# Layer 0 in a front and a back part, three operations moved between engines, and the dense products in one stream

## The chip, the cores and the metric

The kernel runs on one core of a Trainium2 chip. A core has TensorE (PE, matrix products into PSUM), VectorE (DVE), ScalarE (ACT), GpSimd (POOL) and SyncE (SP, which issues transfers). Each engine works through its own queue in order and waits on semaphores for the others. The metric is the device time of one launch in microseconds, lower is better.

## The reference, cut to what matters

Two layers on x of 4 batches x 512 tokens x 256 features, all in float32:

```python
xn = layernorm(x)
# layer 0
q, k, v = xn @ Wq.T + bq, xn @ Wk.T + bk, xn @ Wv.T + bv
ctx  = (elu(q) + 1) * cumsum((elu(k) + 1) * v, over tokens) * 0.25
attn = ctx @ Wo.T + bo
xr   = rms(xn) * norm_w
vals, idx = top_k(xr @ Wc.T / temperature, 32)      # of 512
e    = softmax(vals) @ genes[idx]                   # 32 wide
x    = x + attn + tanh(e @ Wd.T) * xr * (e @ Wu.T) * scale
# layer 1
xn   = layernorm(x)
q, k, v = split(rms(xn) @ w_qkv.T); q, k = rms(q), rms(k); w = exp(k)
y    = sigmoid(q) * cumsum(w * v) / (cumsum(w) + 1e-6)
u, g = split(y @ w_swiglu.T)
a    = xn + (u * silu(g)) @ w_out.T
# two of 16 experts per token, and a shared expert for all
f    = sum over the 2 best experts of weight * swiglu(xn @ w_gate_up[e]) @ w_down[e]
f   += swiglu(xn @ shared_gate_up) @ shared_down
x    = x + a + f
```

## The kernel before

The tokens lie on the 128 partitions; a batch is four tiles of 128 tokens (NT = 4), the residual stream xs stays in the on-chip memory for the whole launch. Every product is done twice over in passes, so that one call of T.matmul appears as two matmuls in the profile.

The work comes as Python generators, each yield ending a step. together() (line 43) draws from several generators in turn, in proportion to the number of steps that each is said to have. What it makes is the order of the program; the framework then places the instructions into the engines' queues, with that order as the priority, and may bring a ready instruction forward.

**layer0(b, i0, nt)** (line 224) is layer 0 for nt tiles of a batch: statistics (bn_stats, line 201; a square root on ACT, line 207; a reciprocal), normalise (line 213, on DVE) to xn, transposes to xnT, then per tile logits (line 286) and top (line 296: four rounds of V.max and V.match_replace over 512 values, then exp into a tile e and a masking product), between them the parts of the attention: attend_kv (phi of k, v, a cumulative scan on DVE, line 271) and attend_q (phi of q, and the context product on DVE, line 280, with the factor QSCALE), then express (line 313: transposes of e, products with genes and with Wd and Wu, tanh, and five products and sums, four of them on POOL) and out (line 336: the output projection, added to xs).

**mix(b, i0, nt)** (line 361) is the attention of layer 1 and the choice of experts: statistics and normalise to xn1, transposes to xn1T, the projections (line 384), copies of q and k on ACT, vs on DVE (line 393), squares, exponentials, transposes and scans (line 421), reciprocals (line 430) and the product yT (line 432), then the expert scores and their two best. Its results go to made[(b, i0)].

**dense(b, half, busy)** (line 566) is, for 256 tokens, everything that is the same for all of them: 11 chunks, three of the shared expert (inputs xn1T, weights sgu and sdn) and eight of the gated product (inputs yT, weights wugt and wot1). A chunk is up (eight matmuls of 256 columns into a PSUM tile gu, tanh on ACT at line 582, a DVE product at line 584, and then, if busy, a copy on ACT and a product on POOL at lines 586 and 587, else one DVE product at line 589) and down (four matmuls into acc at line 595), which follows two chunks behind its up. After the eleventh chunk the two last downs follow at once, and acc, of which there is one buffer (ps_a), is added to xs.

**The stages** (lines 633 to 678): layer 0 of batch 0's first half alone; then mix of it beside layer 0 of the second half; then three stages that each combine a mix, the layer 0 of the next batch and one half of the dense products; then mix of batch 3 beside dense(1, 1) and the loading of the expert weights. After that the routing (route, which works out a row for every token and expert), beside six steps of the dense products of batch 2; the scatter (line 544: 32 indirect transfers issued on POOL, each after the last down emitted before it, see paced, line 92) beside 15 steps of them; and the rest of them. Then come the experts (line 772), each pair of row blocks fetched from xrows on SP (line 709), and last the dense products of batch 3, beside the gathering of the experts' results (line 804) and their addition to xs (line 815).

SP issues the loads of x and of the weights in the order of the program: x of batch 0, the weights of layer 0, those of layer 1 (lines 136 to 147), then x of batches 1 to 3.

Of the kernel before, what the change touches and what calls it, by code (L numbers as in the profile page):

```python
# [53 lines left out]
def tile_two_layers(  # L54
# [79 lines left out]
    nc.sync.dma_start(wot, wo0.rearrange("(h p) e -> p h e", p=P))  # L134

# [12 lines left out]
    for b in range(1, B):  # L148
        load_x(b)
# [5 lines left out]
    for h in range(NH):  # L155
        V.tensor_scalar(wct[:, h], wct[:, h], nwc[:, h : h + 1], None, ALU.mult)
    rtemp = wp.tile([P, 1], F32, name="rtemp")
# [28 lines left out]
    one = first.enter_context(tc.tile_pool(name="one0", bufs=1, side="right"))  # L186
# [7 lines left out]
    def statistics(pool, b, i0, nt):  # L194

        mv = pool.tile([P, NT, 2], F32, name="mv")
        rs = pool.tile([P, 2, NT], F32, name="rs")
        ve = pool.tile([P, NT], F32, name="ve")
        for i in range(nt):
            bs = pool.tile([P, 6], F32, name="bs")  # L200
            V.bn_stats(bs, xs[:, b, i0 + i])
            V.bn_aggr(mv[:, i], bs)
        V.tensor_scalar(rs[:, 0, 0:nt], mv[:, 0:nt, 1], LN_EPS, None, ALU.add)
        V.reciprocal(ve[:, 0:nt], rs[:, 0, 0:nt])
        V.tensor_tensor(ve[:, 0:nt], ve[:, 0:nt], mv[:, 0:nt, 1], ALU.mult)
        V.tensor_scalar(rs[:, 1, 0:nt], ve[:, 0:nt], RMS_EPS, None, ALU.add)
        S.activation(rs[:, :, 0:nt], rs[:, :, 0:nt], AF.Sqrt)
        V.reciprocal(rs[:, :, 0:nt], rs[:, :, 0:nt])
        return mv, rs

    def normalise(to, b, i0, nt, mv, rs):
        for i in range(nt):
            V.tensor_scalar(
                to[:, i], xs[:, b, i0 + i], mv[:, i, 0:1], rs[:, 0, i : i + 1], ALU.subtract, ALU.mult
            )
# [8 lines left out]
    def layer0(b, i0, nt):  # L224

        W = nt * P
        mv, rs = statistics(io, b, i0, nt)
        xn = io.tile([P, NT, D], F32, name="xn")
        normalise(xn, b, i0, nt, mv, rs)

        sl = io.tile([P, 2, NT], F32, name="sl")
        V.tensor_scalar(sl[:, 0, 0:nt], rs[:, 1, 0:nt], rtemp, None, ALU.mult)
        V.tensor_scalar(sl[:, 1, 0:nt], rs[:, 1, 0:nt], scl, None, ALU.mult)
        yield
        xnT = io.tile([P, NH, L], F32, name="xnT")
        for h in range(NH):
            S.copy(xnT[:, h, 0:W], turn(xn, nt, h * P))
        yield


        def project(c):
            pm = bank()[:, 0:W]
            for h in range(NH):
                T.matmul(  # L244
                    pm,
                    wqkv[:, h, c * P : (c + 1) * P],
                    xnT[:, h, 0:W],
                    start=(h == 0),
                    stop=(h == NH - 1),
                )  # L250
            return pm

        def phi(c):

            pm = project(c)
            e = io.tile([P, L], F32, name="phi", bufs=3)[:, 0:W]
            S.activation(e, pm, AF.Relu, bias=nbqk[:, c : c + 1], scale=-1.0)
            S.activation(e, e, AF.Exp, scale=-1.0)
            V.scalar_tensor_tensor(e, pm, bqkv1[:, c : c + 1], e, ALU.add, ALU.max)
            return e  # L260

        ctxT = one.tile([P, NH, L], F32, name="ctxT")
        cums = {}

        def attend_kv(h):
            fk = phi(2 + h)
            pv = project(4 + h)
            kv = one.tile([P, L], F32, name="kv")[:, 0:W]
            V.scalar_tensor_tensor(kv, pv, bqkv[:, 4 + h : 5 + h], fk, ALU.add, ALU.mult)
            cum = io.tile([P, L], F32, name="cum")[:, 0:W]  # L270
            V.tensor_tensor_scan(
                cum, ones[:, 0:W], kv, carry[:, h : h + 1] if i0 else 0.0, ALU.mult, ALU.add
            )
            if i0 + nt < NT:
                V.tensor_copy(carry[:, h : h + 1], cum[:, W - 1 : W])
            cums[h] = cum

        def attend_q(h):
            fq = phi(h)
            V.scalar_tensor_tensor(ctxT[:, h, 0:W], fq, QSCALE, cums[h], ALU.mult, ALU.mult)  # L280


        rden = io.tile([P, NT], F32, name="rden")
        exT = one.tile([P, L], F32, name="exT")

        def logits(i):
            pl = bank()
            for h in range(NH):
                T.matmul(  # L289
                    pl, xnT[:, h, i * P : (i + 1) * P], wct[:, h], start=(h == 0), stop=(h == NH - 1)  # L290
                )
            lg = io.tile([P, NG], F32, name="lg")
            S.copy(lg, pl)  # L293
            return lg

        def top(i, lg):
            tp = io.tile([P, NACT], F32, name="top")
            rep = io.tile([P, NG], F32, name="rep")
            for r in range(NACT // 8):
                src = lg if r == 0 else rep  # L300
                V.max(tp[:, 8 * r : 8 * r + 8], src)  # L301
                V.match_replace(rep, tp[:, 8 * r : 8 * r + 8], src, TAKEN)  # L302
                if r == 0:
                    nm = io.tile([P, 1], F32, name="nm")
                    V.tensor_scalar(nm, tp[:, 0:1], sl[:, 0, i : i + 1], -1.0, ALU.mult, ALU.mult)
                    e = io.tile([P, NG], F32, name="e")
                    S.activation(e, lg, AF.Exp, bias=nm, scale=sl[:, 0, i : i + 1])
            den = io.tile([P, 1], F32, name="den")
            V.scalar_tensor_tensor(e, rep, TAKEN, e, ALU.is_equal, ALU.mult, accum_out=den)
            V.reciprocal(rden[:, i : i + 1], den)  # L310
            return e

        def express(i, e):
# [8 lines left out]
            S.copy(exT[:, i * P : (i + 1) * P], px[:, 0:P])  # L322
            du = bank()
            T.matmul(du, exT[:, i * P : (i + 1) * P], wdut, start=True, stop=True)  # L324
# [8 lines left out]
            G.tensor_tensor(xs[:, b, i0 + i], xs[:, b, i0 + i], bob, ALU.add)  # L333
            G.tensor_tensor(xs[:, b, i0 + i], xs[:, b, i0 + i], dn, ALU.add)

        def out(i):
# [5 lines left out]
            V.tensor_tensor(xs[:, b, i0 + i], ao, xs[:, b, i0 + i], ALU.add)  # L342


        parts = [lambda h=h, f=f: f(h) for h in range(NH) for f in (attend_kv, attend_q)]
        lg = logits(0)
        for i in range(nt):
            nxt = logits(i + 1) if i + 1 < nt else None
            e = top(i, lg)
            yield  # L350
            for part in parts[i * len(parts) // nt : (i + 1) * len(parts) // nt]:
                part()
            yield
            express(i, e)
            lg = nxt
            yield
        for i in range(nt):
# [3 lines left out]
    def mix(b, i0, nt):  # L361
# [17 lines left out]
        for i in range(nt):  # L379
# [13 lines left out]
            V.tensor_scalar(vs[:, i], pv[:, 0:D], rs[:, 1, i : i + 1], None, ALU.mult)  # L393
# [172 lines left out]
    def dense(b, half, busy):  # L566


        unit = (b, 2 * half) if (b, 2 * half) in made else (b, 0)
        t0 = (2 * half - unit[1]) * P  # L570
        ins = [a[:, :, t0 : t0 + HB] for a in made[unit]]
        acc = ps_a.tile([P, 2, D], F32, name="acc")

        def up(gw, g0, uw, u0, m, which, dw, dc):
# [10 lines left out]
            if busy:  # L585
                S.copy(hid[0:m], gu[0:m, 1])  # L586
                G.tensor_tensor(hid[0:m], hid[0:m], th[0:m], ALU.mult)  # L587
            else:
                V.tensor_tensor(hid[0:m], gu[0:m, 1], th[0:m], ALU.mult)
            return hid  # L590

        def down(n, hid):
            m, dw, dc = chunks[n][4], chunks[n][6], chunks[n][7]
            for t in range(2):
# [8 lines left out]
            beat.append(mm.ins.name)  # L603

        hids = []
        for n, c in enumerate(chunks):
            hids.append(up(*c))
            if n >= 2:
                down(n - 2, hids[n - 2])
            yield  # L610
        for n in (NC - 2, NC - 1):
            down(n, hids[n])
        here = xs[:, b, 2 * half : 2 * half + 2]
        V.tensor_tensor(here, acc, here, ALU.add)
        yield


    def chain(*parts):
        for part in parts:
            yield from part  # L620

    H = NC + 1

    def a(b, i0, nt):
        return layer0(b, i0, nt), 2 + 4 * nt

    def m(b, i0, nt):
        return mix(b, i0, nt), 6 + nt

    def d(b, half, busy=True):  # L630
        return dense(b, half, busy), H

    together(a(0, 0, 2))
    together(m(0, 0, 2), a(0, 2, 2))

# [4 lines left out]
    together(m(0, 2, 2), a(1, 0, 4), d(0, 0))  # L640
    together(m(1, 0, 4), a(2, 0, 4), d(0, 1))
    together(m(2, 0, 4), a(3, 0, 4), d(1, 0))
# [27 lines left out]
    together(m(3, 0, 4), d(1, 1), (load_experts(), 17))  # L670
    mixing.close()
    routing = ctx.enter_context(ExitStack())
    d2 = chain(dense(2, 0, False), dense(2, 1, False))
    together((route(), 8), (islice(d2, 6), 6))
    routing.close()

    together((scatter(), 33), (islice(d2, 15), 15))
    run_all(d2)
# [121 lines left out]
    for step, _ in enumerate(chain(dense(3, 0, False), dense(3, 1, False))):  # L800
# [11 lines left out]
        while added < 2 * NTT and 9 * added <= 16 * (step - 4):  # L812
# [61 lines left out]
```

## Time and profile before

| | us |
|---|---|
| three runs, median (lowest, highest) | 592.69 (591.28, 592.82) |
| the profiled execution | 585.74 |
| its span, from the first to the last instruction | 583.9 |

| engine | busy us | share of the span |
|---|---|---|
| PE | 536.5 | 92% |
| DVE | 375.4 | 64% |
| ACT | 233.3 | 40% |
| POOL | 171.7 | 29% |

In the profile a line such as "L578" is a line of the kernel, "gu<-yT,wugt" the tile written and the tiles read, "x512" the number of instructions. The rows of digits cut the span into 40 slices of 14.6 us and give the busy share in tenths (PEclk: the clock granted to PE). The chain of waits is followed back from the last instruction, each step to what released it. The layer stages fill the first 341 us, routing and scatter the next 60, the experts 402 to 522, the last dense products the rest.

### The profile page before, as it was taken

Reading aid. Unit: us, or ns where it says so; the run is one execution under the profiler, and the core shown is the slowest. Engines: PE = TensorE matmul, PEld = TensorE weight load, DVE = VectorE, ACT = ScalarE, POOL = GpSimd, SP = SyncE. Lnnn points to the kernel's source line nnn. Section 1 sums busy time; section 2 is a strip of 40 time slices with the busy share of each in tenths; the row PEclk is TensorE's granted clock in tenths of the full one; section 3 lists DMA queues with packets and bytes.
Section 4 is the critical chain, followed back from the end, with each engine's and each line's share of the span. In section 5 each row is a group of like instructions: output and inputs, shape, how many; then the busy total and the mean of one; then the engine's idle time right before and its main releaser. Section 6 shows DMA issues by size and latency. Waiting matters only on the chain.

```text
span 583.9 us, 7339 instructions
## 1 busy us (share of the span) xinstructions
PE 536.5 (92%) x2384; PEld 393.1 (67%) x2384; DVE 375.4 (64%) x992; ACT 233.3 (40%) x528; POOL 171.7 (29%) x214
## 2 busy tenths in 40 slices
PE   3557999989999999999999999997999999999997
PEld 1334656557555776566777878884777777788886
DVE  4979999998796897968962696331222222225663
ACT  2454745651655716458154511112333333321111
POOL 1234232343222523224251324771000000007760
PEclk9788999999999999999999999998999999999999
DMA  6993000000000000000056611324333333114540
GB/s 164 382 378 137 1 1 1 2 0 1 1 1 0 0 1 2 0 1 1 2 154 193 184 65 54 105 104 135 91 109 108 109 109 99 55 65 116 146 144 28
DMA packets 38453, 47.39 MB, mean 81 GB/s; under 512 B 4016, under 2 KB 34960, under 8 KB 38160
## 3 DMA queue, kind: packets, MB, share of 16 engines
q1 hardware_dynamic: 35344, 38.53, 20.7%
q0 software_dynamic: 3072, 8.39, 4.7%
q8 instruction: 20, 0.33, 0.2%
q14 instruction: 17, 0.14, 0.1%
HBM read 28.30 MB, written 18.61 MB: 80 GB/s over the span
## 4 chain that ended last, share of the span: by engine, by line
PE 53%; DVE 23%; POOL 8%; issue 6%; ACT 6%; DMA 3%; SPq 0%; POOLq 0%; ACTq 0%; DVEq 0%
PE gu L578 10%; PE pu L738 10%; PE py L759 7%; PE acc L595 6%; PE pm L384 5%; PE pt L701 4%; POOL xrows L544 3%; PE pm L244 3%; DVE sums L430 3%; POOL ys L804 3%; DVE rep L302 3%; DVE top L301 3%; PE pm L289 2%; DVE sums L421 2%; PE pm L324 2%
## 5 line engine op out<-in xcount | busy, mean ns | idle before, releaser
L578 PE MATMUL gu<-yT,wugt 128*128 128x256 f32 x512 | 125.6, 382 | 0.0
L578 PEld LDWEIGHTS gu<-yT,wugt 128*128 128x128 f32 x512 | 95.2, 190 | 19.4 <-issue 7.4
L582 ACT ACTIVATE th<-gu 128x256 f32<-128x256 f32 (+1 forms) x88 | 33.3, 382 | 120.0 <-PE gu L578 116.8
L804 POOL DMA_INDIRECT ys<-yrows,slot x32 | 30.4, 949 | 142.0 <-DMA yrows<-yg 129.6
L595 PE MATMUL acc<-wot,hid 128*128 128x256 f32 x256 | 65.3, 382 | 3.1 <-POOL hid L587 2.4
L738 PE MATMUL pu<-wex,xgT 128*128 x188 | 65.0, 468 | 0.8 <-DMA xg<-xrows 0.8
L584 DVE SCALAR_TENSOR_TENSOR th<-th,gu 128x256 f32<-128x256 f32 (+1 forms) x88 | 35.9, 411 | 41.4 <-ACT th L582 41.4
L587 POOL TENSOR_TENSOR hid<-hid,th 128x256 f32<-128x256 f32 (+1 forms) x44 | 33.6, 768 | 95.7 <-ACT hid L586 95.7
L595 PEld LDWEIGHTS acc<-wot,hid 128*128 128x128 f32 x256 | 48.0, 190 | 13.3 <-POOL hid L587 4.5
L747 DVE TENSOR_TENSOR hb<-pu,hb 128x176 f32<-128x176 f32 x47 | 16.0, 341 | 55.7 <-ACT hb L746 55.7
L244 PE MATMUL pm<-xnT,wqkv 128*128 128x512 f32 (+1 forms) x120 | 46.6, 528 | 4.9 <-ACT lg L293 1.9
L384 PE MATMUL pm<-w,xn1T 128*128 128x512 f32 (+1 forms) x128 | 45.5, 498 | 0.0
L578 PE MATMUL gu<-xn1T,sgu 128*128 128x256 f32 (+1 forms) x192 | 45.2, 380 | 0.0
L759 PE MATMUL py<-wex,hgT 128*128 x188 | 44.5, 379 | 0.0
L759 PEld LDWEIGHTS py<-wex,hgT 128*128 128x128 f32 x188 | 35.7, 190 | 8.6 <-issue 0.2
L738 PEld LDWEIGHTS pu<-wex,xgT 128*128 128x128 f32 x188 | 32.5, 193 | 11.2 <-ACT xgT L715 1.0
L384 PEld LDWEIGHTS pm<-w,xn1T 128*128 128x128 f32 x128 | 24.6, 193 | 21.9 <-issue 18.2
L244 PEld LDWEIGHTS pm<-xnT,wqkv 128*128 128x128 f32 x120 | 23.7, 202 | 22.6 <-issue 13.7
L578 PEld LDWEIGHTS gu<-xn1T,sgu 128*128 128x128 f32 (+1 forms) x192 | 34.1, 181 | 6.6 <-issue 0.9
L751 DVE COPY hgT<-pt 128x512 f32<-128x512 f32 (+1 forms) x24 | 16.3, 680 | 34.3 <-PE pt L701 34.3
L544 POOL DMA_INDIRECT xrows<-xn,slot x32 | 30.9, 966 | 19.6 <-DVE cpair L538 9.7
L301 DVE MAX8 top<-rep 128x8 f32<-128x512 f32 x48 | 32.8, 685 | 0.4
(162 smaller groups left out, 879.6 us busy)
## 6 DMA issues: line engine op xcount, KB each, us to landing
xrows<-zero SPq DMA_DIRECT2D x1, 6016.0 KB, 22.6
xg<-xrows SPq DMA_DIRECT2D x23, 256.0 KB, 2.7
yrows<-yg SPq DMA_DIRECT2D x23, 256.0 KB, 2.1
wex<-in_w_gate_up_dram SPq DMA_DIRECT2D x8, 704.0 KB, 4.6
xs<-in_x_dram SPq DMA_DIRECT2D x4, 512.0 KB, 7.9
wugt<-in_wug_dram SPq DMA_DIRECT2D x1, 2048.0 KB, 12.4
wex<-in_w_down_dram SPq DMA_DIRECT2D x4, 512.0 KB, 5.1
out_dram<-xs SPq DMA_DIRECT2D x7, 256.0 KB, 2.8
```

The costliest lines, as they stand in the source:

```text
L244: T.matmul(pm, wqkv[:, h, c * P : (c + 1) * P], xnT[:, h, 0:W], start=(h == 0), stop=(h == NH - 1),)
L301: V.max(tp[:, 8 * r : 8 * r + 8], src)
L384: T.matmul(o[:, 0:n], xnT[:, h, i * P : (i + 1) * P], w1[:, h, at : at + n], start=(h == 0), stop=(h == NH - 1),)
L544: sc = G.indirect_dma_start(out=xrows, out_offset=bass.IndirectOffsetOnAxis(ap=slot[:, k, i : i + 1], axis=0), in_=xn1[:, i // NT, i % NT] ...
L578: T.matmul(gu[0:m, k], w[:, h, at : at + m], ins[which][:, h], start=(h == 0), stop=(h == NH - 1))
L582: S.activation(th[0:m], gu[0:m, 0], AF.Tanh, scale=0.5)
L584: V.scalar_tensor_tensor(th[0:m], th[0:m], 1.0, gu[0:m, 0], ALU.add, ALU.mult)
L587: G.tensor_tensor(hid[0:m], hid[0:m], th[0:m], ALU.mult)
L595: mm = T.matmul(acc[:, t], hid[0:m, t * P : (t + 1) * P], dw[0:m, dc], start=(n == 0 and t == 0), stop=(n == NC - 1), skip_group_check=True,)
L738: T.matmul(pg[:, 0 : 2 * NI], xT[:, i, h], wex[:, bass.ds(at[i] + h * 2 * NI, 2 * NI)], start=(h == 0), stop=(h == NH - 1),)
L759: mm = T.matmul(py[:, i * D : (i + 1) * D], hT[:, i, h], wex[:, bass.ds(at[i] + EW - (2 - h) * D, D)], start=(h == 0), stop=(h == 1),)
L804: G.indirect_dma_start(out=ys[:, asked], out_offset=None, in_=yrows, in_offset=bass.IndirectOffsetOnAxis(ap=slot[:, k, n : n + 1], axis=0) ...
```

## The change

Layer 0 becomes two generators. front(b, wide) does a whole batch: statistics, xn, xnT, all logits (kept in lg, six buffers), the attention up to the context. back(b, i0, nt) does the top-32, express and out for some of its tiles. Fronts of batches 0 and 1 run ahead of the first dense products and take their projections' PSUM from the tiles gu (wide). Batch 0's back and mix are still in halves. The scan no longer needs a carry in layer 0; cum has one buffer instead of two, kv takes the place of phi's tile, exp works in place on lg, exT is a tile of its own.

xn (in both layers) and vs go from DVE to ACT, for which statistics works out -mean times the reciprocal deviation with one small DVE operation more. The context product goes from DVE to POOL, QSCALE into wot once at the start. x of batch 1 is loaded ahead of layer 1's weights.

The dense products are one generator over all eight halves: down follows two chunks behind up across the halves' ends, and acc is added as soon as the eleventh down is emitted. The choice between POOL and DVE for the second product goes by a flag that is set before routing. Of its 88 chunks 3 + 2 + 3 + 9 + 2 + 3 + 2 + 9 + 2 + 5 = 40 are placed in the mixing, 5 beside route, 15 beside scatter, 6 behind, and 22 at the end; before, it was 44 in the mixing, 22 from routing to the experts and 22 at the end. The pace of the last additions is set anew for 22 steps instead of 24.

```diff
+    load_x(1)
     w1 = const.tile([P, NH, 3 * D + NE], F32, name="w1")
...
-    for b in range(1, B):
+    for b in range(2, B):
         load_x(b)
...
+    S.mul(wot, wot, QSCALE)
...
+        V.scalar_tensor_tensor(mv[:, 0:nt, 0], mv[:, 0:nt, 0], -1.0, rs[:, 0, 0:nt], ALU.mult, ALU.mult)
         return mv, rs
...
-            V.tensor_scalar(
-                to[:, i], xs[:, b, i0 + i], mv[:, i, 0:1], rs[:, 0, i : i + 1], ALU.subtract, ALU.mult
+            S.activation(
+                to[:, i], xs[:, b, i0 + i], AF.Identity, bias=mv[:, i, 0:1], scale=rs[:, 0, i : i + 1]
             )
...
+    def front(b, wide):
...
+            if wide:
+                pm = ps_d.tile([P, 2, HB], F32, name="gu").rearrange("p i c -> p (i c)")
+            else:
+                pm = bank()
...
+            kv = phi(2 + h)
             pv = project(4 + h)
+            V.scalar_tensor_tensor(kv, pv, bqkv[:, 4 + h : 5 + h], kv, ALU.add, ALU.mult)
+            cums[h] = io.tile([P, L], F32, name="cum", bufs=1)
+            V.tensor_tensor_scan(cums[h], ones, kv, 0.0, ALU.mult, ALU.add)
...
-            V.scalar_tensor_tensor(ctxT[:, h, 0:W], fq, QSCALE, cums[h], ALU.mult, ALU.mult)
+            G.tensor_tensor(ctxT[:, h], fq, cums[h], ALU.mult)
...
+        for h in range(NH):
+            for i in (2 * h, 2 * h + 1):
+                logits(i)
+                yield
+            attend_kv(h)
+            yield
+            attend_q(h)
+            yield
+
+    def back(b, i0, nt):
...
+        top(i0)
+        yield
+        for i in range(i0, i0 + nt):
+            if i + 1 < i0 + nt:
+                top(i + 1)
+                yield
+            express(i)
             yield
+        for i in range(i0, i0 + nt):
             out(i)
             yield
...
-            V.tensor_scalar(vs[:, i], pv[:, 0:D], rs[:, 1, i : i + 1], None, ALU.mult)
+            S.activation(vs[:, i], pv[:, 0:D], AF.Identity, scale=rs[:, 1, i : i + 1])
...
+        for half in range(2 * B):
...
+            for n, c in enumerate(chunks):
+                behind.append((half, n, up(ins, bool(calm), *c)))
+                if len(behind) > 2:
+                    down(*behind.pop(0))
+                yield
...
+    f0, f1 = front(0, True), front(1, True)
+    b0 = back(0, 0, 2)
+    run_all(islice(f0, 4))
+    together(some(f0, 6), some(b0, 2))
+    together(some(b0, 4), some(f1, 2))
+    m0 = mix(0, 0, 2)
+    next(m0)
+    run_all(islice(f1, 3))
+    together((m0, 7), some(f1, 5))
...
+    together((back(0, 2, 2), 6), d(3))
+    m0 = mix(0, 2, 2)
+    next(m0)
+    run_all(islice(dd, 2))
+    together((m0, 7), d(3))
+    together((back(1, 0, NT), 12), (front(2, False), 10), d(9))
+    m1 = mix(1, 0, NT)
+    next(m1)
+    run_all(islice(dd, 2))
+    together((m1, 9), (back(2, 0, NT), 12), (front(3, False), 10), d(3))
+    m2 = mix(2, 0, NT)
+    next(m2)
+    run_all(islice(dd, 2))
+    together((m2, 9), (back(3, 0, NT), 12), d(9))
...
+    together((m3, 9), d(5), (load_experts(), 17))
     mixing.close()
     routing = ctx.enter_context(ExitStack())
+    calm.append(True)
+    together((route(), 8), d(5))
     routing.close()
+    together((scatter(), 33), d(15))
+
+    run_all(islice(dd, 6))
...
-        while added < 2 * NTT and 9 * added <= 16 * (step - 4):
+        while added < 2 * NTT and 17 * added <= 32 * (step - 3):
```

## The prediction

> **What bounds it now.** I read engine totals first, then the slices, then busy time by stretch, then the chain of waits where the stretches show a hole.
>
> ```profile
> span 583.9 us, 7339 instructions
> PE 536.5 (92%) x2384; PEld 393.1 (67%) x2384; DVE 375.4 (64%) x992; ACT 233.3 (40%) x528; POOL 171.7 (29%) x214
> PE   3557999989999999999999999997999999999997
> DVE  4979999998796897968962696331222222225663
> PEclk9788999999999999999999999998999999999999
> ```
>
> PE (TensorE) is above nine tenths from the sixth slice (14.6 us each) on; only the first four or five have room. But 92% is not 92% at peak: one 128x256 matmul is listed at 382 ns, while the chain shows how closely they follow:
>
> ```profile
> 86.54 1.29 PE gu L578 x6
> 98.51 2.63 PE pm L384 x8
> 137.87 1.73 PE gu L578 x8
> ```
>
> Eight 256-wide ones take 1.73 us, 216 each; the eight of L384 (four 512 wide, four 272 wide) 2.63, so 430 and 230. Priced so (L738 296, transposes 109 ns, 0.22 us for one tile's eight small ones of L321), the 2384 matmuls are 512 us of work in a span of 584: **72 us lost**, idle or at a low clock. By start times, 35.7 are gone at 60 us, 40.4 at 85, 58.2 at 341, 65.2 at 410, and hardly any in the experts (410 to 520). The stretches say why:
>
> ```profile
> 0.00:30.00 30.00, 14.31 (x44) 8.32 (x45) 21.14 (x72) 9.16 (x18) 6.35 (x17) 0.89 0.85 275
> 30.00:60.00 30.00, 19.21 (x68) 11.54 (x67) 26.53 (x88) 15.02 (x35) 11.13 (x15) 0.84 0.69 242
> 60.00:90.00 30.00, 27.52 (x131) 18.52 (x129) 29.84 (x94) 19.04 (x40) 8.39 (x12) 0.99 0.00 1
> 90.00:190.00 100.00, 95.97 (x397) 60.66 (x398) 86.73 (x228) 52.12 (x118) 32.14 (x41) 1.00 0.00 1
> 341.00:398.00 57.00, 56.70 (x263) 49.00 (x261) 29.68 (x75) 8.05 (x21) 33.20 (x39) 1.00 0.21 74
> 398.00:402.00 4.00, 0.63 (x4) 0.42 (x4) 0.42 (x1) 0.28 (x1) 0.00 (x0) 0.98 0.61 174
> ```
>
> Columns: length, then PE, weight loads, DVE (VectorE), ACT, POOL busy, clock, DMA. To 60 us PE has 33.5 of 60, at a granted 0.84 to 0.89, while DVE has 47.7: the top-32 search (four rounds of L301 and L302, starting 0.66 us apart, some 6.2 us a tile) keeps PE from work. The dense products fill PE once they exist; the first on yT starts at 84.7. To 341 us PE has 283 of work and DVE 280 busy: nearly tied. At 398 PE stands again, and the chain tells for what:
>
> ```profile
> 395.57 2.41 DMA xrows<-xn,slot
> 399.05 3.30 DMA xg<-xrows
> 402.36 2.71 PE pu L738 x4
> ```
>
> The last scatter is issued at 395.57, the fetch waits for it, and the expert matmuls for the fetch; the dense chunks have run out at 397.5.
>
> **Start, the largest part.** Before, batch 0's first half must pass layer0 and mix before any chunk can run, beside the second half's top-32. After, PE has the fronts of two batches to run meanwhile. A front is 24 projections and 16 logits at 430 ns and 8 transposes: 18.1 us. Two of them 36.2; back(0,0,2) 2 x 2.4 (4 transposes, L321, 2 x 430, 4 x 216); mix(0,0,2) 2 x 3.5; the three shared chunks, which need xn1T alone, 3 x 2.59. Together 55.8 us of work without yT. When is yT there? DVE needs f0's statistics 3, two top-32 12.4, f0's phi, kv and scans 6.2, dn and out 1.9, f1's statistics and phi 9.2, mix up to yT 13.5 (2 statistics, 11.5 scans, reciprocals, products): 46. It begins at 4.3, the first lg is at 14 now (one larger statistics chain: say 14.5), and the serial stretch from the second top-32 to exp(k) (8.7 us from the end of L309 at 29.7 to xs at 38.4 now, then statistics, square root, qkv, squares, root, exp) leaves holes that f1 fills only in part. I take 72 for yT instead of 84.7. If PE ran all 55.8 by then, 16 would be lost; I take 22 (it starts near 10.8, and f1's statistics come after two top-32), against 40.4 lost before. The gain is **18**, bounds 8 and 24. Part is clock: in 23 to 29.8, 40 to 46.9 and 57 to 60.5 the granted clock was 0.5 and PE busy 12.6, so 6.3 were lost by it, after idle stretches of 5 and 5.8 us.
>
> load_x(1) goes ahead of the seven weight loads from w1 on in SP's queue: 0.43 us of issue, and 0.5 MB at the 381 GB/s of that stretch is 1.4 us for w1, whose first matmul is at 48.9. Hidden. The multiplication of wot is one 512-wide ACT (0.62, L637).
>
> **Engines changed in the mixing.**
>
> ```profile
> L213 DVE TENSOR_SCALAR xn<-xs,mv,rs 128x256 f32<-128x256 f32 x32 | 15.2, 525 | 0.2
> L410 ACT ACTIVATE qk<-qk,cf 128x256 f32<-128x256 f32 x16 | 8.0, 509 | 0.0
> L280 DVE SCALAR_TENSOR_TENSOR ctxT<-phi,cum 128x512 f32<-128x512 f32 x6 | 4.1, 688 | 0.1
> L368 POOL TENSOR_TENSOR xs<-xs,xn 128x512 f32<-128x512 f32 x2 | 2.6, 1322 | 8.2 <-DVE xn L213 8.2
> ```
>
> DVE loses L213 15.2, vs (L393) 7.6 and the context product 4.1 + 1.6: 28.5. It gains one small product per statistics, 9 x 0.2 = 1.8. ACT's normalise has two pointer operands; L410, SBUF to SBUF with one, is the near row: 32 x 509 = 16.3. The Trainium skill ("ScalarE: Activation LUTs", What ACT_TABLE_LOAD costs) adds about 93 ns for each pointer operand: 32 x 602, an estimate of 19.3. vs costs 16 x 473 (L326) = 7.6. ACT goes from 173 busy of 341 to 197 or 200; either sum fits, and I take the row. Square roots stay one per statistics, and the same table switches (1.28 us) with them.
>
> The skill speaks against the product on POOL: "GPSIMD Engine Reference", Engine selection, puts elementwise two-input work on VectorE, GPSIMD being about 2x slower. The rows agree (1322 against 688): the engines' sum grows. "SBUF — State Buffer", two separate sides, is worse: the two share a port pair as an exclusive lock, the loser waiting out the whole instruction. By the rule 8 x 1.32 = 10.6 of DVE could be blocked. The trace:
>
> ```profile
> 68.60 0.73 POOL L412 TENSOR_TENSOR vs<-vs,qk 128x256 f32<-128x256 f32 x1 [15.60 <-ACT qk L410]
> 68.71 0.65 DVE L408 TENSOR_SCALAR cf<-cf 128x2 f32<-128x2 f32 x1
> ```
>
> L408 ends with the POOL operation; undisturbed it takes 0.15. But most DVE operations here read PSUM or one operand, and L213, which pays it most (525 mean, 384 least: 4.5 us), goes. Between 0 and 10.6 I take 4.
>
> Sum to 341: DVE 280 - 28.5 + 1.8 + 4 - 1.6 (four chunks less) = 256; PE 283 - 10.4 = 272. So DVE drops below PE. But top-32 is put off: after the start DVE has some 210 left and PE 222, 0.95, where from 85 to 341 it was 208 to 238, 0.87. The mixing lost 17.8 there; I charge **4 more**, bounds -4 and 14.
>
> **Chunks beside routing.** The same 33 chunks lie between the third mixing and the experts: 11 + 22 before, 7 + 26 after. But of the 26 chunks 67.3 us stand beside routing and scatter, where 22 gave 57. Scatters follow each other at 1.265 us (0.96 and 0.30 issue), 40.5 for 32; from the start of routing, 341.5, to the first takes 14.2, and to the first fetched rows 60.5. After, that ends 6.8 before the chunks do. The 3.4 us idle, the half clock behind it (0.5 in 402 to 405) and the serial first pair lose 6.8 now: **gain 5**, bounds 0 and 7.
>
> **One stream.** down(10) of a half no longer follows its own up at once (0.64 us idle at 549.4); seven such places: gain 1 to 3. Against it, the next half's first down waits for DVE's addition on the single acc with one up (1.73 us) between instead of three. Addition 0.68 and its hand-over fit if DVE is free. Net **gain 1**, bounds -3 and 3. In the last part the additions follow their gathers by 2.2 to 3 chunks instead of about 4; gather and landing take 1.3 + 3.3, within 5.8 us, so nothing.
>
> **Sum:** 18 - 4 + 5 + 1 = 20. The profiled execution took 585.7 (span 583.9 and 1.8 around it): 565.7. The runs' median is 592.7, 7 above that execution, and the forecast is for such runs: 592.7 - 20, rounded down to **572**.
>
> **Rivals.** *VectorE takes it back.* Mix 1, back 2 and front 3 come together with 5 chunks: about 60 us of DVE, 55 of PE. If mix waits there and in the next stage, 12 of the start's gain return: 584. For it: DVE at 29.84 of 30 after the start. Against: 28.5 us less in sum.
>
> *The order doesn't arrive.* Queue order isn't program order (L441's memset, late in the program, ran at 2.00 us): chunks may be pulled forward, the scatter gap stay and half the start's gain fail: 592.7 - 9 + 3 = 587.
>
> *Slower: POOL's queue.* cum has one buffer; the second scan of a front waits on DVE for the context product of the first half, and POOL takes its queue in order. Ahead of a product can stand dn or hid, whose waits were 47.9 us in 12 and 95.7 in 27, some 4 each, 12.6 at most. Behind the scan stand phi and the next top-32. At 4 for each of 8 the loss is 32, the sum 12 slower: 605. From 2.5 us per product the gain is gone. Against: POOL is 29% busy, and DVE's queue can have other work placed ahead of the scan.
>
> **Chances.** Forecast 0.57, VectorE 0.16, order 0.09, POOL's queue 0.15, nothing measurable (within 0.3%, 1.8 us, what this kernel's measurement tells from none) 0.03. The forecast's own range is 560 to 581; the first two rivals reach 590, and 557 takes in the start's upper bound. Faster: 0.57 and nearly all of 0.25.
>
> **What will show it.** Right: PE busy over 42 in the first 60 us, first yT chunk before 75; no idle PE between dense and pu; DVE's sum near 353; lost time near 52. Wrong: a scan waiting on ctxT, hid waits grown, DVE full with PE under 90% from 100 to 280, chunks spent before the scatter ends.

## The result, and the profile after

The changed kernel is slower: 600.48 us (597.45 to 601.21) against 592.24 us (591.28 to 592.82) of the kernel before, measured beside it, a ratio of 1.0135, 95% interval 1.0117 to 1.0153. The forecast was 572 us. Measured again later, beside its variants, it took 591.80 us (590.90 to 592.08) against 587.50, a ratio of 1.0076 (1.0059 to 1.0092).

The page of the changed kernel, with the same rows as before:

```profile
span 597.2 us, 7258 instructions
PE 538.2 (90%) x2360; PEld 388.1 (65%) x2360; DVE 352.2 (59%) x930; ACT 255.0 (43%) x566; POOL 176.9 (30%) x218
PE   2958898999999989899899399879999999999987
DVE  2899999598874859934932983232222222225563
PEclk9998999999999999999989889999999999999999
```

DVE's sum fell by 23 us, as worked out (353 was forecast). But PE's row has a 3 in its 23rd slice (328 to 343 us), where it had a 9 before, and the granted clock (PEclk) has an 8 in the 24th. By stretches (length, then PE, weight loads, DVE, ACT, POOL busy, clock, DMA):

```profile
0.00:30.00 30.00, 19.52 (x43) 8.82 (x44) 17.00 (x51) 13.53 (x22) 6.97 (x17) 1.00 0.78 271
30.00:60.00 30.00, 20.89 (x76) 10.24 (x74) 29.29 (x92) 20.90 (x37) 9.61 (x12) 0.94 0.70 245
90.00:190.00 100.00, 95.25 (x419) 65.67 (x418) 74.33 (x212) 57.64 (x124) 39.23 (x50) 1.00 0.00 1
333.00:350.00 17.00, 7.25 (x21) 5.64 (x20) 15.03 (x22) 0.38 (x1) 2.29 (x7) 0.70 0.00 0
```

In the first 60 us PE is busy 40.4 instead of 33.5: the start did gain, but under the 42 named in the prediction. From 90 to 190 DVE has a quarter of its time free, and PE is no fuller than before. From 333 to 350 PE stands for more than half of the time, while DVE is busy 15 of 17 us. What DVE does there is told by the timeline of the same execution (start, duration, instruction, idle time before and its releaser), first DVE, then PE, and then DVE of the kernel before at the same place, cut to four lines:

```profile
332.29 1.21 DVE L426 TENSOR_TENSOR_SCAN sums<-ones,pm 128x512 f32<-128x512 f32 x1
333.42 3.34 DVE L435 RECIPROCAL sums<-sums 128x256 f32<-128x256 f32 x2
336.68 0.63 DVE L433 SCALAR_TENSOR_TENSOR sums<-pm,sums 128x512 f32<-128x512 f32 x1
337.22 0.68 DVE L437 TENSOR_TENSOR yT<-sums 128x512 f32<-128x512 f32 x1
337.82 3.36 DVE L435 RECIPROCAL sums<-sums 128x256 f32<-128x256 f32 x2
341.09 1.16 DVE L426 TENSOR_TENSOR_SCAN sums<-ones,pm 128x512 f32<-128x512 f32 x1
342.17 0.40 DVE L589 SCALAR_TENSOR_TENSOR th<-th,gu 128x256 f32<-128x256 f32 x1
```

```profile
332.34 1.46 PE L583 MATMUL gu<-yT,wugt 128*128 128x256 f32 x6
343.56 1.22 PE L603 MATMUL acc<-wot,hid 128*128 128x256 f32 x2 [9.75 <-DVE hid L591]
```

```profile
331.75 3.34 DVE L430 RECIPROCAL sums<-sums 128x256 f32<-128x256 f32 x2
335.01 0.36 DVE L584 SCALAR_TENSOR_TENSOR th<-th,gu 128x256 f32<-128x256 f32 x1
...
338.71 0.41 DVE L584 SCALAR_TENSOR_TENSOR th<-th,gu 128x256 f32<-128x256 f32 x1
339.03 3.36 DVE L430 RECIPROCAL sums<-sums 128x256 f32<-128x256 f32 x2
```

From 329.5 to 342.2 DVE's queue holds only the scans, reciprocals and products of mix(3). The first th (L589), which a dense chunk needs before its PSUM tile comes free, is behind them; before, a th stood between the reciprocals. Three chunks wait for their th, one in each of the three tiles gu. PE's next instruction is a down (L603) that needs the hid (L591) made from that th, so PE stands for 9.75 us. The granted clock is 0.57 from 343.5 to 350 us, just behind that. L591 is the second product of the chunks emitted after the flag is set, so the chunks that wait are already those placed behind the mixing, and the 40 placed in it have been used up.

Priced as in the prediction (216 ns for a 256-wide matmul, and so on), both kernels have the same 512 to 513 us of PE work; what is lost beside it, by stretch, in us:

| stretch | before (span 583.9) | changed, first execution (597.2) | changed, second execution (590.0) | second minus before | forecast |
|---|---|---|---|---|---|
| to 80 | 40.0 | 31.3 | 31.5 | -8.5 | -18 |
| 80 to 330 | 16.8 | 25.5 | 25.1 | +8.3 | +4 |
| 330 to 360 | 1.7 | 13.6 | 13.3 | +11.6 | none |
| 360 to 420 | 6.4 | 7.6 | 1.5 | -4.9 | -5 |
| 420 to the end | 6.2 | 6.5 | 5.9 | -0.3 | -1 |

At 330 us both kernels have lost the same, 57 us: what the start gains is gone again by the end of the mixing.

The two executions of the changed kernel differ in one stretch. In the first, ACT began several of its th 3 to 6 us after their gu between 370 and 395 us; the second shows nothing of it, nor does any variant. Why it came is open, and the experiments are read against the second.

### The profile page after: what moved, and what is told of

It reads as the page before. It is cut to its first block, busy times and chain, and to the rows that moved or that the text cites. A ratio compares the mean times of both kernels' runs of the same rounds, so it can differ in the third digit from the quotient of the medians.

```text
span 597.2 us, 7258 instructions
## 1 busy us (share of the span) xinstructions
PE 538.2 (90%) x2360; PEld 388.1 (65%) x2360; DVE 352.2 (59%) x930; ACT 255.0 (43%) x566; POOL 176.9 (30%) x218
## 4 chain that ended last, share of the span: by engine, by line
PE 56%; DVE 28%; ACT 6%; issue 3%; DMA 3%; POOL 3%; SPq 0%; another core or an unknown queue 0%; DVEq 0%; ACTq 0%; POOLq 0%
PE gu L583 16%; PE pu L767 9%; PE acc L603 9%; PE py L788 7%; DVE rep L312 5%; DVE top L311 5%; PE pm L389 4%; PE pt L730 3%; DVE sums L435 3%; DVE sums L426 3%; PE pm L224 2%; PE pm L334 1%; DVE lg L318 1%; DMA wqkv<-in_wqkv_dram 1%; DVE bs L203 1%
## 5 line engine op out<-in xcount | busy, mean ns | idle before, releaser
L583 PEld LDWEIGHTS gu<-yT,wugt 128*128 128x128 f32 x512 | 96.8, 192 | 17.9 <-ACT hid L593 3.4
L603 PE MATMUL acc<-wot,hid 128*128 128x256 f32 x256 | 68.7, 386 | 13.4 <-DVE hid L591 11.8
L589 DVE SCALAR_TENSOR_TENSOR th<-th,gu 128x256 f32<-128x256 f32 (+1 forms) x88 | 36.1, 413 | 71.8 <-ACT th L587 60.1
L767 PE MATMUL pu<-wex,xgT 128*128 x188 | 63.8, 461 | 0.8 <-ACT xgT L744 0.8
L603 PEld LDWEIGHTS acc<-wot,hid 128*128 128x128 f32 x256 | 47.4, 192 | 21.4 <-DVE hid L591 12.6
L594 POOL TENSOR_TENSOR hid<-hid,th 128x256 f32<-128x256 f32 (+1 forms) x40 | 29.7, 751 | 64.0 <-ACT hid L593 63.9
L583 PE MATMUL gu<-xn1T,sgu 128*128 128x256 f32 (+1 forms) x192 | 47.8, 383 | 0.4 <-DVE phi L264 0.4
L389 PE MATMUL pm<-w,xn1T 128*128 128x512 f32 (+1 forms) x128 | 44.0, 493 | 0.5 <-ACT xn1T L377 0.5
L283 PE MATMUL pm<-wct,xnT 128*128 128x512 f32 x64 | 32.5, 641 | 1.1 <-ACT xnT L242 1.1
L311 DVE MAX8 top<-rep 128x8 f32<-128x512 f32 x48 | 32.6, 680 | 0.2
L312 DVE MATCH_REPLACE8 rep<-top,rep 128x512 f32<-128x512 f32 x48 | 32.3, 674 | 0.0
```

The lines of the kernel that those rows point to most:

```text
L283: T.matmul(pl, xnT[:, h, i * P : (i + 1) * P], wct[:, h], start=(h == 0), stop=(h == NH - 1))
L389: T.matmul(o[:, 0:n], xnT[:, h, i * P : (i + 1) * P], w1[:, h, at : at + n], start=(h == 0), stop=(h == NH - 1),)
L583: T.matmul(gu[0:m, k], w[:, h, at : at + m], ins[which][:, h], start=(h == 0), stop=(h == NH - 1))
L589: V.scalar_tensor_tensor(th[0:m], th[0:m], 1.0, gu[0:m, 0], ALU.add, ALU.mult)
L603: mm = T.matmul(acc[:, t], hid[0:m, t * P : (t + 1) * P], dw[0:m, dc], start=(n == 0 and t == 0), stop=(n == NC - 1), skip_group_check=True,)
L767: T.matmul(pg[:, 0 : 2 * NI], xT[:, i, h], wex[:, bass.ds(at[i] + h * 2 * NI, 2 * NI)], start=(h == 0), stop=(h == NH - 1),)
```

## The experiments

They ran in four groups, each on a chip of its own and beside the kernel before: e1 to e4, then c0 and e5 to e7, then e8 to e11, then e12 to e14. The kernel before took 587.05 to 587.50 us in each. Across groups the ratios are compared. The times expected for e1 to e4 start from the 600.5 us of the first measurement, so they too are judged by the ratios and the traces. "44, 26, 18" means the number of chunks placed in the mixing, from routing to the experts, and at the end; the changed kernel has 40, 26, 22.

| label | edit to the changed kernel | us | ratio to before (95%) |
|---|---|---|---|
| c0_after | none | 591.80 | 1.0076 (1.0059-1.0092) |
| e1_44_22 | 44, 22, 22 | 588.18 | 1.0015 (1.0003-1.0028) |
| e2_40_shifted | four chunks later within the mixing | 589.64 | 1.0048 (1.0031-1.0065) |
| e3_calm_late | flag set after route | 592.45 | 1.0100 (1.0080-1.0119) |
| e6_44_26_18 | 44, 26, 18 | 583.01 | 0.9925 (0.9909-0.9942) |
| e4_xn_vs_dve | xn, vs on DVE | 586.69 | 0.9993 (0.9982-1.0003) |
| e7_44_22_dve | e1 and e4 | 584.30 | 0.9955 (0.9937-0.9972) |
| e8_44_26_18_dve | e6 and e4 | 579.24 | 0.9869 (0.9832-0.9905) |
| e5_ctx_dve | context product on DVE | 597.75 | 1.0169 (1.0139-1.0199) |
| e9_hold_top | e6, searches held | 589.20 | 1.0046 (1.0034-1.0059) |
| e10_hold_dve | e8, searches held | 587.14 | 1.0009 (0.9990-1.0029) |
| e11_front1_early | e6, front(1) earlier | 584.87 | 0.9955 (0.9936-0.9974) |
| e13_front1_late | e8, front(1) later and not wide | 590.39 | 1.0073 (1.0050-1.0097) |
| e12_drain | e8, half ends as before | 580.75 | 0.9909 (0.9882-0.9936) |
| e14_slack | e8, first down later | 578.54 | 0.9862 (0.9843-0.9880) |

**The kernel alone.**

> The changed kernel unaltered, beside its variants and the kernel before. All theories: about 1.012 to 1.015 of the kernel before of the same call, with a hole of some 10 us in PE at 333 us. Open is whether the late ACT instructions seen between 370 and 395 us in its profile (some 6 us) come again: if they do, they belong to this kernel; if not, they were of that execution.

The hole came again, 9.75 us long, and the late th did not. The ratio of 1.0076 is under the 1.012 to 1.015 expected.

**The hole at the end of the third mixing.** Theory A: 40 chunks are too few for the mixing. The framework brings ready chunks forward, so that they are used up before mix(3) ends, and the long DVE run then has no th between its instructions; the number in all counts, not the place. Theory B: the flag calm, set before routing, gives the second products to DVE just when it has the least room.

```diff
-    together((m3, 9), d(5), (load_experts(), 17))     # e1 (and 2 instead of 6 behind the scatter)
+    together((m3, 9), d(9), (load_experts(), 17))
...
-    together((m2, 9), (back(3, 0, NT), 12), d(9))     # e2: d(5) here, d(9) beside m3
+    together((m2, 9), (back(3, 0, NT), 12), d(5))
...
-    calm.append(True)                                 # e3
     together((route(), 8), d(5))
+    calm.append(True)
```

> Edit: four more chunks beside mix of batch 3 (9 instead of 5 in the last step list), four fewer after the scatter (2 instead of 6), so 44 in the mixing and 22 beside routing as before, all else as changed. Theory A (too few chunks before the end of mix 3 in the program, so that VectorE's scans and reciprocals stand in one unbroken run and the chunks' th operation waits behind them): the idle PE of about 10 us at the end of mix 3 falls below 2 and the half clock behind it goes, 13 us; the wait of PE for the first fetched rows comes back, 3 to 5; time 590 to 593 against 600.5. Theory B (chunks of the calm kind, whose second product is on VectorE, stall PE): the stall only moves behind the 44th chunk; 597 to 601.

> Edit: the same 40 and 26 chunks, but 5 instead of 9 beside mix 2 and back 3, and 9 instead of 5 beside mix 3. Theory A in the form that the number of chunks in the program before the end of mix 3 decides (ready chunks are pulled forward, so by then the 40 are used up wherever they stand): the stall stays, 8 to 10 us; 598 to 602. Rival: the place decides, the stall goes; 587 to 592.

> Edit: the flag that sends the chunks' second product to VectorE is set behind routing instead of before it, so the five chunks beside routing use ScalarE and GpSimd for it. Theory A: the stall at the end of mix 3 stays 8 to 12 us of idle PE, because th, which is on VectorE in either kind, waits in the same place; only the name of the last releaser changes; 597 to 602. Theory B: the stall goes, 587 to 590.

With 44 chunks the hole is gone (lost from 330 to 360 us: 3.8). With 40 it stays wherever they are put, 8.0 us in e2, and also with the flag set later, 9.2 us in e3, where the instruction waited for is another but the th behind it the same. PE of e2, then of e3:

```profile
341.29 1.22 PE L603 MATMUL acc<-wot,hid 128*128 128x256 f32 x2 [8.02 <-DVE hid L591]
```

```profile
341.61 1.22 PE L583 MATMUL gu<-yT,wugt 128*128 128x256 f32 x2 [9.21 <-ACT hid L593]
```

B is out. By the ratios e2 may be 0.3% faster than the changed kernel; the intervals just overlap. In e1 the four chunks are missing at the scatter instead. PE of e1:

```profile
396.56 1.03 PE L603 MATMUL acc<-wot,hid 128*128 128x256 f32 x4
401.03 0.80 PE L730 MATMUL pt<-ident,xg 128*128 128x128 f32 x4 [3.44 <-DMA xg<-xrows]
```

This is the old gap, and 5.5 us are lost from 400 to 420. So the four chunks should come from the end, which has 22:

```diff
-    together((m3, 9), d(5), (load_experts(), 17))     # e6
+    together((m3, 9), d(9), (load_experts(), 17))
...
-        while asked < 2 * NTT and 5 * asked <= 9 * step:
+        while asked < 2 * NTT and 9 * asked <= 20 * step:
...
-        while added < 2 * NTT and 17 * added <= 32 * (step - 3):
+        while added < 2 * NTT and 9 * added <= 20 * (step - 3):
```

> 44 chunks in the mixing, 26 from routing to the experts, 18 at the end. Theory A: the hole at the end of the third mixing goes (lost time from 330 to 360 us under 4 us) and the scatter's gap stays covered (lost time from 400 to 420 us under 2 us), so that the whole is 10 to 13 us faster than the changed kernel and 3 to 6 faster than the one with 44 and 22. Rival 'the end needs its chunks': the gathers and additions come to stand alone behind the last chunk and give back the 5 us at the end.

It is 8.8 us under the changed kernel on the same chip, where 10 to 13 was expected, and faster than the kernel before. The stretch from 330 to 360 us, of the kernel before, then of the changed kernel (second execution), then of e6:

```profile
330.00:360.00 30.00, 28.82 (x139) 24.50 (x138) 27.74 (x57) 4.95 (x13) 7.56 (x14) 1.00 0.24 79
```

```profile
330.00:360.00 30.00, 19.54 (x83) 15.61 (x82) 26.90 (x53) 2.13 (x6) 5.38 (x10) 0.83 0.13 37
```

```profile
330.00:360.00 30.00, 27.83 (x125) 22.18 (x126) 27.70 (x56) 4.64 (x13) 7.93 (x14) 1.00 0.29 84
```

DVE does about as much in all three; PE does 8.3 us more in e6 than in the changed kernel. DVE's order in e6 shows why:

```profile
331.82 3.34 DVE L435 RECIPROCAL sums<-sums 128x256 f32<-128x256 f32 x2
335.07 0.36 DVE L589 SCALAR_TENSOR_TENSOR th<-th,gu 128x256 f32<-128x256 f32 x1
...
338.77 0.41 DVE L589 SCALAR_TENSOR_TENSOR th<-th,gu 128x256 f32<-128x256 f32 x1
339.10 3.35 DVE L435 RECIPROCAL sums<-sums 128x256 f32<-128x256 f32 x2
342.37 0.36 DVE L589 SCALAR_TENSOR_TENSOR th<-th,gu 128x256 f32<-128x256 f32 x1
```

Now each pair of reciprocals, 3.3 us, is followed by a th, as in the kernel before, and PE gets a tile back in time. At the scatter 1.8 us are lost from 400 to 420, so the gap stays covered. Behind 420 us e6 loses 1.1 more than the changed kernel, so the end hardly misses its four chunks. An edit that keeps 40 chunks and gives their th a place between the reciprocals was not run.

**Operations moved between engines.** The edits put xn and vs, or the context product, back on DVE.

```diff
-            S.activation(to[:, i], xs[:, b, i0 + i], AF.Identity, bias=mv[:, i, 0:1], scale=rs[:, 0, i : i + 1])   # e4, e7, e8 (and no -mean)
+            V.tensor_scalar(to[:, i], xs[:, b, i0 + i], mv[:, i, 0:1], rs[:, 0, i : i + 1], ALU.subtract, ALU.mult)
...
-            S.activation(vs[:, i], pv[:, 0:D], AF.Identity, scale=rs[:, 1, i : i + 1])
+            V.tensor_scalar(vs[:, i], pv[:, 0:D], rs[:, 1, i : i + 1], None, ALU.mult)
...
-            G.tensor_tensor(ctxT[:, h], fq, cums[h], ALU.mult)     # e5
+            V.tensor_tensor(ctxT[:, h], fq, cums[h], ALU.mult)
```

> Edit: xn and vs back on VectorE, as before the change, without the extra small product; the context product stays on GpSimd. Theory C (the normalise on ScalarE delays the transposes, and with them the start and the mixes): the time lost by PE between 80 and 330 us falls from 25 to about 17, and PE's wait for xn at 40 us by 2; 590 to 594. If C is wrong and VectorE's load matters: it rises, 601 to 608. The stall at the end of mix 3 isn't touched by either.

> 44 chunks in the mixing and 22 after it, xn and vs on DVE. Theory A: the hole at the end of the third mixing goes here too, 7 to 9 us under the variant with xn and vs on DVE and 40 chunks, so some 579 us where the kernel before takes 587. Rival (DVE's share decides): with 23 us more on DVE the chunks' products are late all the same, and the time stays at 586 to 588.

> 44, 26 and 18 chunks, xn and vs on DVE. If both gains add up (8.8 us by the placing of chunks, 5 us by xn and vs on DVE): 578 where the changed kernel takes 592 and the kernel before 587. If DVE's share decides: 583.

> Context product back on DVE. Theory A (the loss is the run of DVE work at the end of the third mixing, which no product of a dense chunk interrupts): little changes, within 3 us of the changed kernel, the hole at 333 us stays at 8 to 10 us. Rival 'POOL's queue': the scans no longer wait for POOL, the mixing from 80 to 330 us loses 16 us as before instead of 25, and the whole is 8 us faster than the changed kernel.

Moving xn and vs to ACT costs time. The pairs stand in different groups, so by their ratios: 1.0076 against 0.9993 (e4), 1.0015 against 0.9955 (e7), 0.9925 against 0.9869 (e8), which is 0.6 to 0.8% or 3 to 5 us in each, although DVE has 12 us more to do in e8 than in e6 (362.9 against 350.4 by their pages). Where the time goes is not where e4 looked for it. With xn and vs on DVE, PE loses 2.1 to 2.4 us less up to 80 us in each pair. From 80 to 330 us it loses 1.5 and 1.1 less in e7 and e8, but 2.3 more in e4 (27.7 where about 17 was expected). The hole is not touched by it: 9.2 us in e4, none in e7. e7 stopped at 584 where 579 was expected, since the scatter's gap is open again in it (3.5 us at 393 us); e8, which covers both, gives the sum of both gains and is faster than either kernel.

The context product is the other way round: on DVE the whole is 6.0 us slower, which neither expectation had. PE loses 1.6 us more up to 80 us and 4.6 more from 80 to 330. Its rows, in e5 and in the changed kernel:

```profile
L278 DVE TENSOR_TENSOR ctxT<-phi,cum 128x512 f32<-128x512 f32 x8 | 6.1, 761 | 0.1
```

```profile
L278 POOL TENSOR_TENSOR ctxT<-phi,cum 128x512 f32<-128x512 f32 x8 | 10.2, 1271 | 45.6 <-DVE phi L264 23.5 <-DVE rden L319 16.0 <-DVE lgt L397 6.1
```

POOL takes 1.7 times as long for each, but it has the time. In the changed kernel no scan waits for ctxT; what waits for it is DVE's xs, 0.9 us in two, a weight load of PE, 1.4 us in one, and a memset on POOL itself (wex), 7.1 us in one. But four of the eight products on POOL hold up an operation of DVE that runs beside them. One of them, in the changed kernel's second execution:

```profile
37.43 1.27 POOL L278 TENSOR_TENSOR ctxT<-phi,cum 128x512 f32<-128x512 f32 x1 [8.08 <-DVE rden L319]
37.73 0.98 DVE L338 TENSOR_TENSOR cf<-rden,sl 128x1 f32<-128x1 f32 x1
```

cf ends with the product at 38.7 us; half of the sixteen cf take 0.16 us or less. Against the medians of their kind the four are 2.9 us longer in all. That fits DVE's sum, which is 4.0 us more in e5 (356.5 against 352.5) and not 6.1.

**The start.** The first chunk on yT starts at 91 us in the changed kernel, not at 72. DVE's timeline to the last yT of mix(0, 0, 2), at 87 us, has 25 rounds of the search (L311), over six tiles' worth at four each. Two tiles were needed, so that four searches of 6.2 us, of batch 0's other half and of batch 1, went ahead of it, though the program has them behind. Theory C: this order costs the start. e9 and e10 give the first V.max of every later search a place behind that yT in DVE's queue (an order, no wait); e11 draws the first two steps of front(1) beside front(0); e13 puts front(1) behind mix(0, 0, 2).

```diff
+                if r == 0 and held:                                   # e9, e10
+                    tc.add_manual_dep(first_max.ins, held[-1], order_only)   # held: the first yT's instructions
...
-    together(some(f0, 6), some(b0, 2))                                # e11
-    together(some(b0, 4), some(f1, 2))
+    together(some(f0, 6), some(b0, 2), some(f1, 2))
+    run_all(islice(b0, 4))
...
-    f0, f1 = front(0, True), front(1, True)                           # e13
+    f0, f1 = front(0, True), front(1, False)
...
-    together(some(b0, 4), some(f1, 2))
-    m0 = mix(0, 0, 2)
-    next(m0)
-    run_all(islice(f1, 3))
-    together((m0, 7), some(f1, 5))
+    run_all(islice(b0, 4))
+    run_all(mix(0, 0, 2))
...
-    together((back(0, 2, 2), 6), d(3))
+    together((back(0, 2, 2), 6), (f1, 10), d(3))
```

> The variant with 44, 26 and 18 chunks, and in it no search of the top 32 (but the two of batch 0's first half) ahead of batch 0's first yT in DVE's queue. Theory C (the first yT comes at 87 instead of 72 us because some four further searches, 25 us, were brought ahead of it): the first chunk on yT starts at 73 to 78 us instead of 91, and the lost time at 100 us falls from 32 to about 24; the whole is 4 to 8 us faster than without it, 575 to 579. Rival D (the start is bound by the sum of DVE's work, whatever its order): the first yT comes early, but the searches are missing later, lost time at 330 us stays at 56, and the whole at 583.

> 44, 26 and 18 chunks, xn and vs on DVE, and the searches held behind the first yT. Theory C: 4 to 8 us below the same without the hold. Rival D: no difference, or slower, since DVE has 23 us more to do.

> 44, 26 and 18 chunks, and batch 1's statistics and xn taken from beside the end of back(0, 0, 2) to beside front(0). Theory C: PE's hole of 5 us at 41 us is filled by batch 1's logits, the lost time at 60 us falls by 3 to 5, but the first yT comes no earlier than 88 us, so that the whole gains 3 us at most. If the late xn of batch 1 was what cost the start (rival): the lost time at 100 us falls by 8 and the whole by 6 or more.

> 44, 26 and 18 chunks, xn and vs on DVE, and front(1) not ahead of the first dense products but beside back(0, 2, 2) and the next three chunks. Theory S (front(1) fills PE in the start, which is where the start's gain is from): the lost time at 80 us rises from 29 to 38 or more, the first yT comes at 80 or earlier, and the whole is 5 to 9 us slower. Rival (the start is the sum of DVE's work, and front(1) only moves it): the lost time at 120 us is within 3 of the same, the whole within 3.

Theory C fell, and its rival came nearer. In e9 yT does come earlier (first chunk at 80.9 us) and the lost time at 80 us is 4.3 less than in e6, but it is 5.6 more at 100 us, and the whole is some 7 us slower by the ratios; e10 is 8 us slower than e8. PE of e9 shows where it goes:

```profile
82.68 1.46 PE L593 MATMUL gu<-yT,wugt 128*128 128x256 f32 x6
90.21 1.09 PE L333 MATMUL pm<-ident,lg 128*128 128x128 f32 x4 [6.07 <-DVE lg L326]
```

PE's own order has batch 0's second half next, and the search that was put off is now what it waits for. e11 filled part of the hole at 41 us (3.0 us less lost at 60 us than in e6), and at 100 us it was all given back. e13 shows what the second front is worth: without it ahead, yT comes at 76 us and the whole is 11 to 12 us slower than e8. (Its projections no longer use the tiles gu either, which was not run apart.) PE of e13:

```profile
39.61 1.89 PE L348 MATMUL pm<-wot,ctxT 128*128 128x256 f32 x8
50.27 1.13 PE L223 MATMUL pm<-ident,xn 128*128 128x128 f32 x4 [8.77 <-DVE xn L215]
```

So the split gives PE work while DVE is full, as it was said to do. e9 and e10 fit a start that is bound by DVE's sum: what was put off there was missing a little later.

**The half ends of the one stream.** e12 lets the two last downs follow the eleventh up at once, as before; e14 puts off only a half's first down by one more chunk.

```diff
-                if len(behind) > 2:
+                while len(behind) > (0 if n == NC - 1 else 2):            # e12
+                while len(behind) > (3 if behind[0][1] == 0 else 2):      # e14, with five tiles hid
                     down(*behind.pop(0))
```

> 44, 26 and 18 chunks, xn and vs on DVE (579.2 in its own call, 0.987 of the kernel before), and at each half's end the two last downs follow the eleventh up at once, as in the kernel before. If one stream gains, as the prediction had it: 1 to 3 us slower. Rival E (what the mixing loses more than before, 8 us from 80 to 330, comes from the next half's first down, which waits for the addition on the single acc): the gaps ahead of that down go, and the whole is 2 to 5 us faster.

> 44, 26 and 18 chunks, xn and vs on DVE, and only the first down of a half put off by one more chunk (five tiles hid instead of four), so that the addition on the single acc has two chunks' ups beside it. Rival E: the gaps ahead of the first down go (1.4 to 2.3 us at 2 to 4 half ends), 2 to 5 us faster. Otherwise: within 1.5 us.

Neither differs from e8 by more than the intervals allow (0.9909 and 0.9862 against 0.9869). In the lost time from 80 to 330 us, 24.5 in e8, they stand within 2 us of it: the wait on the single acc is not what the mixing loses.

## Why the prediction was wrong

The sum was 20 us faster; the profiled executions (spans 583.9 and 590.0) lie 6.1 the other way. Of these 26 us, 11.6 are a hole that the sum does not have, 9.5 the start, 4.3 the mixing, and less than 1 the rest. (The runs on one chip lie only 4.3 us apart, so that the parts are sure to a us or two.)

**Chunks beside routing: the step that failed.** The gain it named came, to a tenth: 4.9 us from 360 to 420, and the experts follow without a gap. But the step had the bounds 0 and 7 and took the four chunks out of the mixing for nothing. The prediction counted them as 1.6 us less for DVE and 10.4 less for PE, as sums of the stage. That mix(3) ends in 13 us of DVE work in a row, which PE outlasts only if th of dense chunks stand between, was not looked for; the kernel before has the same reciprocals (L430, 3.34 us for two) with a th between, and this was there to be read. It cost 11.6 us, and giving the four chunks back (e6) brought 8.8. By the stage's sums, which were all that it looked at, DVE stood under PE.

**Start: the term yT at 72 us was mis-sized.** The gain is 8.5, not 18. DVE's list of 46 us ahead of yT held only what yT needs. The queue held the searches of four more tiles, 25 us, as well: DVE was busy 73.8 us until yT came at 87.7, and the first chunk on it began at 91. That order alone would cure it is refuted by e9 and e10: DVE's work of the start is needed soon after, too. xn and vs on ACT take 2.1 to 2.4 us of the start's gain. That the second front fills PE was right (e13).

**Mixing: charged 4, measured 8.3.** The sign and the bounds held. xn and vs on ACT account for some 4 us of the whole in three pairs, where "either sum fits" had them at nothing, but for 1.5 us at most of these 8.3. ACT's duration was nearer to the estimate of 602 ns, made with the 93 ns that the Trainium skill ("ScalarE: Activation LUTs", What ACT_TABLE_LOAD costs) gives for one more pointer operand, than to the row taken (509): the changed kernel's L216 has a mean of 590. The row of L410 had one pointer operand too few. The rest of the 8.3 is open: the layer stages' last matmul on pm starts at 332.1 us (333.5 before), although DVE is busy 26 us less until then, so that PE's earlier start hardly brings the mixing's end forward. Moving the context product back, holding searches, or easing the half ends did not cure it; a cause is not shown.

**Context product on POOL.** 4 us of DVE were charged for the shared port, between 0 and 10.6. Measured are some 2.9 us in four products, so this term was right in kind and size, and the worst case of the rule did not come. As a whole the move is a gain of 6.0 us (e5), more than the 4.0 by which it shortens DVE's sum; why more is not shown.

**One stream: forecast 1.** The stretch behind 420 us, where only the last one or two of the seven half ends lie, has 0.3. e12, which takes it back everywhere, is 0.4% slower than e8, but the intervals overlap, so a gain is not shown.

**Rivals.** "The order doesn't arrive" had the mechanism, chunks brought forward and half of the start's gain lost, but it expected them to be missing at the scatter; they were missing one stage earlier, where 40 instead of 44 stand. "POOL's queue", which carried the chance of slower, did not happen. "VectorE takes it back" looked at the wrong view: DVE was at 0.73 to 0.74 from 90 to 290 us, and what counted was 13 us in which nothing else came between.

## What to carry to other kernels

Before work that fills one engine is moved from a stage to another, look in the stage that loses it for the longest run of instructions on the engine that hands it back its buffers, and compare that run with what the buffers hold; the sums of the stage do not show it. When a framework may bring work forward, a count per stage is only the count in all: take fillers from where they are not missed (here the end), and check both ends of the stage. And an earlier start is worth only what is left of it some stages later: here 8.5 us gained at 80 us were gone at 330.

## What the hardware showed beyond that

A product of 512 columns took 1271 ns on POOL and 761 on DVE, and four of the eight on POOL held up a DVE operation, 2.9 us in all; still the version with POOL was 6.0 us faster. The granted clock of PE was 0.70 in the 17 us that began with the hole, and from 330 to 360 us 13.3 us were lost, of which the hole itself is 9.75. The kernel before took 592.2 us in the first measurement and 587.1 to 587.5 on the four chips of the experiments, which is as much as several of the effects here, so that times of different groups are compared by their ratios alone.
